# Packing every ninth sample with masked multiply-adds on VectorE, to the last channel, in a convolve-and-whiten kernel

## The chip, the cores and the metric

The kernel runs on one core of one Trainium2 chip. The metric is the device time of one execution in microseconds (us); less is better. The engines named below are PE (TensorE), DVE (VectorE), ACT (ScalarE), POOL (GpSimd) and SP (SyncE, which here only issues DMAs). SBUF is the memory on the chip, with 128 partitions; PSUM is the memory into which PE writes, in eight banks.

## What is computed

The input x is [4 images, 64 channels, 256, 256] in float32. Two layers follow each other.

```python
# layer 0: a long 2-D convolution for each channel, with a separable kernel
hx = implicit_filter(z, X weights)            # small sine network, 256 taps x 64 channels
hy = implicit_filter(z, Y weights)
k  = einsum('ijk,imk->ijmk', hx, hy)[0]       # one 256x256 kernel per channel, an outer product
y  = irfft2(rfft2(x, 512) * rfft2(k, 512) / 512)[..., :256, :256]
x  = y + x * bias[:, None, None]

# layer 1: whitening over channels
x1   = transpose(x, (1, 0, 2, 3)).reshape(64, -1)       # channels x (image, row, column)
x1_s = x1[:, ::9]                                       # every ninth sample
mean1 = mean(x1_s, axis=-1)
cov  = x1_s @ x1_s.T / n + 0.01 * eye(64)
out  = newton_schulz_inverse_sqrt(cov, 5) @ (x1 - mean1)
```

## The kernel before

An image of one channel is held as 128 partitions x 2 row blocks x 256 columns: row b*128 + p lies in partition p, block b. Eight channels of one image are one x tile; there are four such tiles. The list `steps` holds 32 steps of (group g of eight channels, image n). The first 24 go through groups 0 to 5, all images of each; the last eight go image by image through groups 6 and 7. Inside a step the loop takes two channels at a time (c = 0, 2, 4, 6).

The convolution is two products with Toeplitz matrices on PE, one along each axis. `group` (products at L220) does the second product of one pair of channels and the first product of a pair two items later, so that PE always has both. The first product is copied to SBUF by ACT (L409). The second is added to x * bias by DVE (L412), which writes the result over x in its tile. The very first and last pairs have no partner, and are done alone by `half_group` (PE at L252, DVE's addition at L289). `store` then sends the result to DRAM in two DMAs on SP (y_d, L425).

**Packing.** The whitening needs every ninth sample, for a sum of products over samples. The sample that an index belongs to depends on image, row and column, so that in each partition and row block one residue s of 0 to 8 is the right first column. The tile samp of an image is [128, 2 blocks, 29 samples, 65] and holds in its last column ones. For each s, DVE copies the columns s, s + 9, ... of x into it where an integer mask for (partition, image, block, s) is not zero (COPY_PREDICATED, L319, in `pack_ops`). One operation takes both row blocks and eight channels (four in groups 6 and 7): nine operations a tile, or nine for each half of a tile.

These operations are not emitted at once. `store` puts them on a list, todo, with a planned cost, and `pack(time)` adds time to a credit and emits from the list until the credit is used up. `group` calls pack(2.92) at its end; at the very end each of the last two pairs calls pack(1.0) between `half_group` and `store`, and a last pack() empties the list. The cost of an operation is `0.3 + 1.5e-3 * H2 * NJ * channels`, with H2 = 2 and NJ = 29.

The last four channels of the last step are packed otherwise: `pack_by_pe` multiplies the tile's columns on PE with nine selection matrices (pick, the identity scaled by the mask, made on ACT at L135 in the second step), two channels at a time, and ACT (and DVE for one copy) bring the sums from PSUM into samp (L309, L311).

**After the loop.** `covariance(n)` sums the products of samp of image n on PE (L333). Images 0 to 2 have theirs inside the last steps, image 3 behind the loop. Products named spin (L442) are dummy matmuls on PE, two instructions each. `whitening` is a chain of small products and DVE/ACT operations that ends in the matrix W and a shift. Then 32 pieces of the stored convolution (2 MB each) are read back (yi, L357), multiplied by W (L635), shifted by ACT and DVE (L639, L640), and written out (L645). The first 13 read-backs take the places of tiles that are done with: nine are issued in the last steps of the loop and four behind the covariance in program order, all on SP's queue, behind the stores.

The order on each engine is the order of the program; nothing is reordered by a scheduler.

Of the kernel before, what the change touches and what calls it, by code (L numbers as in the profile page):

```python
# [37 lines left out]

F32 = mybir.dt.float32
I32 = mybir.dt.int32  # L40
AF = mybir.ActivationFunctionType
ALU = mybir.AluOpType
AX = mybir.AxisListType
# [2 lines left out]
NB, C, L = 4, 64, 256  # L46
P, H2 = 128, 2
EMB, ORDER = 33, 64
PIX = L * L
CG = 8  # L50
HP = P // 2
STEP = 9
NJ = 29
NSAMP = (NB * PIX + STEP - 1) // STEP
EPS = 0.01
N_ITER = 5
GW = P + L
FP = 4096

TURN = 6.283185  # L60
# [4 lines left out]
def conv_whiten_kernel(ctx: ExitStack, tc: tile.TileContext, a: dict, out: bass.AP):  # L65
    nc = tc.nc
    x = a["x"]

    const = ctx.enter_context(tc.tile_pool(name="const", bufs=1))
# [6 lines left out]
    psA = ctx.enter_context(tc.tile_pool(name="psA", bufs=8, space=bass.MemoryType.PSUM))  # L76

    y_d = [dram.tile([H2 * C, PIX // H2], F32, tag=f"y{n}", name=f"y_d{n}") for n in range(NB)]
    g_d = dram.tile([P, GW], F32, tag="g", name="g_d")
    g0_d = dram.tile([2 * CG, GW], F32, tag="g0", name="g0_d")  # L80

# [12 lines left out]
    wbd = scratch[:, 0:2, :].rearrange("p a w -> p (a w)")[:, 0 : 3 * P]  # L94
    nc.sync.dma_start(out=wbd, in_=a["wbd"])
    decay = scratch[:, 15, :]
    mask = const.tile([P, NB, H2, STEP], I32, tag="mask", name="mask")
    bias = const.tile([P, C], F32, tag="bias", name="bias")

    def load_x(t, g, n, c):  # L100
# [6 lines left out]
    steps = [(g, n) for g in range(C // CG - 2) for n in range(NB)]  # L107
# [10 lines left out]
    ident = const.tile([P, P], F32, tag="ident", name="ident")  # L118
    make_identity(nc, ident)
    samp = []  # L120
    for n in range(NB):
        t = spool.tile([P, FP], F32, tag="samp", name=f"samp{n}")
        samp.append(
# [3 lines left out]
        nc.gpsimd.memset(samp[n][:, :, NJ - 1, 0:C], 0.0)  # L127


    rows = const.tile([P, STEP], F32, tag="rows", name="rows")  # L130
    pick = const.tile([P, STEP, P], F32, tag="pick", name="pick")

    def load_pick(lo, hi):
        for s in range(lo, hi):
            nc.scalar.activation(pick[:, s, :], ident, AF.Copy, scale=rows[:, s : s + 1])  # L135

    taps = scratch[:, 11:13, :].rearrange("p a w -> p (a w)")[:, 0:GW]
    nc.gpsimd.memset(taps[:, L:GW], 0.0)  # L140

# [35 lines left out]
    nc.sync.dma_start(out=g0_d[0:CG], in_=taps[0:CG])  # L177
    nc.scalar.dma_start(out=g0_d[CG:], in_=taps[ORDER : ORDER + CG])
    nc.gpsimd.dma_start(out=g_d, in_=taps)
    nc.gpsimd.tensor_copy(rows, mask[:, NB - 1, 0, :])  # L180
    busy(22)

    def new_toeplitz(g):
# [4 lines left out]
    def load_toeplitz(t, g, f, half, lo=0, hi=CG, issue=nc.sync):  # L188
# [7 lines left out]
                tensor=source.tensor,  # L196
                offset=source.offset + row * GW + skip,
                ap=[[1, HP], [GW, hi - lo], [1, L - skip]],
            ),
# [91 lines left out]
                        ALU.mult, ALU.add,  # L291
                    )

    def pack_by_pe(g, n, yt, cs):

        pk = psA.tile([P, H2, cs.stop - cs.start, NJ], F32, tag="psA", name=f"pk_{cs.start}")
        for s in range(STEP):
            for b in range(H2):
                nj = (L - s + STEP - 1) // STEP
                nc.tensor.matmul(  # L300
                    pk[:, b, :, 0:nj],
                    lhsT=pick[:, (s - b) % STEP, :],
                    rhs=yt[:, cs, b, s : s + STEP * (nj - 1) + 1 : STEP],
                    start=(s == 0 and b == 0),
                    stop=(s == STEP - 1 and b == H2 - 1),
                    skip_group_check=True,
                )
        dst = samp[n][:, :, :, g * CG + cs.start : g * CG + cs.stop]
        nc.scalar.copy(dst[:, 0], pk[:, 0].rearrange("p c j -> p j c"))  # L309
        copy = nc.vector.tensor_copy if cs.stop == CG else nc.scalar.copy  # L310
        copy(dst[:, 1], pk[:, 1].rearrange("p c j -> p j c"))  # L311

    def pack_ops(g, n, yt, cs):
        def op(s):
            nj = (L - s + STEP - 1) // STEP
            src = yt[:, cs, :, s : s + STEP * (nj - 1) + 1 : STEP].rearrange("p c b j -> p b j c")
            dst = samp[n][:, :, 0:nj, g * CG + cs.start : g * CG + cs.stop]
            m = mask[:, n, :, s : s + 1].unsqueeze(3).to_broadcast([P, H2, nj, cs.stop - cs.start])
            nc.vector.copy_predicated(dst, m, src)  # L319

        cost = 0.3 + 1.5e-3 * H2 * NJ * (cs.stop - cs.start)
        return [(cost, lambda s=s: op(s)) for s in range(STEP)]

    cov = const.tile([P, C + 1], F32, tag="cov", name="cov")
    nc.gpsimd.memset(cov, 0.0)
# [38 lines left out]
    todo = []  # L364
# [55 lines left out]
    def store(second):  # L420
        g, n, c, yt, _ = second
        halves = g >= C // CG - 2
        for b in range(H2):
            row = b * C + g * CG + c
            nc.sync.dma_start(  # L425
                out=y_d[n][row : row + 2, :].rearrange("c (p w) -> p c w", w=L),
                in_=yt[:, c : c + 2, b],
            )

        if c == CG - 2 and (g, n) != steps[-1]:  # L430
            todo.extend(pack_ops(g, n, yt, slice(CG // 2 if halves else 0, CG)))
        elif c == CG // 2 - 2 and halves:
            todo.extend(pack_ops(g, n, yt, slice(0, CG // 2)))
# [3 lines left out]
    def spin(times):  # L437

        p = psA.tile([P, P], F32, tag="psA", name=f"spin{len(spins)}")
        spins.append(p)  # L440
        for _ in range(times):
            nc.tensor.matmul(p, lhsT=ident, rhs=ident, start=True, stop=True)  # L442
# [114 lines left out]
    with tc.manual_schedule(  # L557
        engines={engines.PE, engines.SP, engines.DVE, engines.Activation, engines.Pool}
    ):
        toep = {0: new_toeplitz(0)}  # L560

        for f, lo, hi in ((0, 0, 2), (0, 2, 4), (0, 4, 6), (1, 0, 2), (0, 6, 8), (1, 2, 4), (1, 4, 8)):
            for half in range(2):
                load_toeplitz(toep[0], 0, f, half, lo, hi, nc.scalar if half else nc.sync)
        for c in range(0, CG, 2):
            load_x(x_tiles[1], *steps[1], c)
        for i, (g, n) in enumerate(steps):
            xt = x_tiles[i % 4]
            for c in range(0, CG, 2):
                item = (g, n, c, xt, [])  # L570
                if g == C // CG - 1 and n > 0 and c == 2:
                    covariance(n - 1)
                if len(pending) == 2:
                    group(item, pending.pop(0))
                else:
                    half_group(item, 0)
                pending.append(item)
                if i == 0 and c == 6:

                    fold = const.tile([P, C], F32, tag="fold", name="fold")  # L580
                    nc.vector.tensor_tensor(fold, ident[:, 0:C], ident[:, C:P], ALU.add)

                    nc.scalar.activation(bf[:, 0:1], samp[0][:, 0, 0, C : C + 1], AF.Sqrt)
                if i == 1 and c < CG - 2:
                    load_pick(c // 2 * 3, c // 2 * 3 + 3)

                if i + 2 < len(steps):
                    load_x(x_tiles[(i + 2) % 4], *steps[i + 2], c)
                if (i, c) in blocks:
                    tg, part = blocks[i, c]  # L590
                    if part == 0:
                        toep[tg] = new_toeplitz(tg)
                    lo = part % 2 * CG // 2
                    load_toeplitz(toep[tg], tg, part // 4, part // 2 % 2, lo, lo + CG // 2)
                for _ in range(early.get((i, c), 0)):
                    load_next()
        g, n, c, yt, _ = pending[0]
        for item in pending:
            half_group(item, 1)
            pack(1.0)  # L600
            store(item)

        pack()
        i15 = place(2 * C, rows=C).rearrange("p (u c) -> p u c", u=2)
        for u in range(2):
            nc.gpsimd.tensor_scalar(i15[:, u], ident[0:C, 0:C], 1.5, None, ALU.mult)  # L606
        ones = place(P, rows=C)
        nc.gpsimd.memset(ones, 1.0)
        for lo in range(CG // 2, CG, 2):
            pack_by_pe(g, n, yt, slice(lo, lo + 2))  # L610
        spin(4)
        covariance(NB - 1)
        while len(loaded) < len(homes):
            load_next()
        W, shift = whitening(i15, ones)
# [3 lines left out]
    for i, (n, q) in enumerate(pieces):  # L619
        yt = loaded.pop(i)  # L620
# [5 lines left out]
        for w in range(FP // 1024):  # L626
# [6 lines left out]
            for k in range(2):  # L633
                for u in range(2):
                    nc.tensor.matmul(  # L635
                        po[u][halves[k]], lhsT=W[halves[u]], rhs=v[halves[u], k, cols],
                        start=True, stop=True,
# [12 lines left out]
def _constants():  # L650


    import numpy as np

    t = np.linspace(0.0, 1.0, L).astype(np.float32)
    lo, hi = math.log(0.01) / 1.5, math.log(0.01) / 0.3
    deltas = np.linspace(lo, hi, C).astype(np.float32)
    d = np.exp(-(t[None, :] * np.abs(deltas)[:, None]).astype(np.float64))
    decay = np.concatenate([d / (2 * L), d])[:, ::-1].astype(np.float32)
    p, n, b, s = np.ogrid[0:P, 0:NB, 0:H2, 0:STEP]  # L660
    mask = ((n * PIX + (b * P + p) * L + s) % STEP == 0).astype(np.int32)
    return {"decay": decay, "mask": mask}


# [41 lines left out]
```

## Time and profile before

| | us |
|---|---|
| median of 3 runs | 903.47 |
| lowest and highest run | 902.69, 903.47 |
| span of the profiled execution, first to last instruction | 902.1 |
| PE busy | 781.2 |
| DVE busy | 581.5 |
| ACT busy | 395.5 |
| POOL busy | 14.5 |
| COPY_PREDICATED at L319, 351 instructions | 297.2 |
| selection products at L300, 72 instructions | 8.3 |

The profiled execution's own time is not listed apart; the runs lie 0.6 to 1.4 us above its span.

The page of the profile gives, for 40 equal slices of the span, each engine's busy share in tenths (9 is 90% or more), the clock granted to PE (PEclk) and the DMA engines' share. The chain that ended last is followed back from the last instruction, at each step to what released it; a line of it in order of time has the start, the length, what ran, and how many instructions. A line of the timeline has the start and length of a run of like instructions on one engine, with their count. A line of the windows has, for one stretch, its length, then the busy time and number of instructions of PE, PEld, DVE, ACT and POOL, then the granted clock, the DMA share and GB/s.

### The profile page before, as it was taken

How to read it: one execution, taken by the hardware profiler on the slowest of the kernel's cores; microseconds unless marked ns; L12 is line 12 of the kernel's file. 1: busy time of each engine (PE TensorE's matmuls, PEld its weight loads, DVE VectorE, ACT ScalarE, POOL GpSimd, SP SyncE). 2: the span in 40 equal slices, each digit the busy share in tenths (PEclk: the TensorE clock that was granted, in tenths of full speed). 3: DMA queues.
4: the chain of work that ended last, by engine and by line, in shares of the span. 5: the costliest groups of instructions: out<-in, count | busy, mean ns of one | idle time of the engine just before them, and what ended most of it. 6: DMA issues, size and time to landing. Idle time of an engine off the chain costs nothing.

```text
span 902.1 us, 28046 instructions
## 1 busy us (share of the span) xinstructions
PE 781.2 (87%) x11928; PEld 647.5 (72%) x11928; DVE 581.5 (64%) x801; ACT 395.5 (44%) x676; POOL 14.5 (2%) x40
## 2 busy tenths in 40 slices
PE   8999999999999999999999999999999565666200
PEld 7999999999999999999999999999533111212000
DVE  3487778877888778877888877877688332233200
ACT  2655554545455555545454444442487232233200
POOL 1000000000000000000000000000010000000000
PEclk9999999999999999999999999999999766866755
DMA  7988889798788888888997899979999999999998
GB/s 209 327 262 252 242 261 271 234 273 251 247 263 261 244 264 259 258 250 267 293 275 241 285 351 356 335 237 390 375 401 429 430 432 432 429 434 430 430 430 355
DMA packets 117912, 285.61 MB, mean 317 GB/s; under 512 B 8891, under 2 KB 91116, under 8 KB 110108
## 3 DMA queue, kind: packets, MB, share of 16 engines
q1 hardware_dynamic: 113436, 244.94, 79.0%
q0 software_dynamic: 3056, 37.95, 10.0%
q8 instruction: 95, 1.56, 0.7%
q10 hardware_dynamic: 1296, 0.93, 0.4%
q14 instruction: 29, 0.24, 0.1%
HBM read 149.35 MB, written 134.44 MB: 315 GB/s over the span
## 4 chain that ended last, share of the span: by engine, by line
PE 74%; DMA 11%; another core or an unknown queue 7%; DVE 0%; issue 0%; SPq 0%; ACT 0%; POOLq 0%; DVEq 0%
PE p L220 64%; DMA out_dram<-yi 5%; DMA yi<-y_d 5%; PE po L635 4%; PE pc L333 2%; PE ph L252 1%; PE pk L300 1%; PE spin L442 1%; DMA toep<-g_d 0%; PE busy L152 0%; PE pm L158 0%; SPq L357 0%; DMA scratch<-in_zw_dram 0%; DVE yi L640 0%
## 5 line engine op out<-in xcount | busy, mean ns | idle before, releaser
L220 PE MATMUL p<-toep,x 64*64 64x64 f32 (+3 forms) x5040 | 579.5, 284 | 0.8 <-issue 0.8
L220 PE MATMUL p<-toep,o 64*64 64x64 f32 (+3 forms) x5040 | 579.5, 284 | 0.0
L220 PEld LDWEIGHTS p<-toep,x 64*128 64x128 f32 (+1 forms) x5040 | 535.7, 166 | 24.4 <-issue 1.3
L220 PEld LDWEIGHTS p<-toep,o 64*128 64x128 f32 (+1 forms) x5040 | 536.7, 166 | 10.7 <-issue 0.2
L409 ACT COPY o<-p 64x512 f32<-64x512 f32 x504 | 292.8, 581 | 294.2 <-PE p L220 286.6
L319 DVE COPY_PREDICATED samp<-mask,x 128x464 f32<-128x464 int32 (+3 forms) x351 | 297.2, 847 | 9.8 <-DVE x L412 0.2
L412 DVE SCALAR_TENSOR_TENSOR x<-x,bias,p 128x512 f32<-128x512 f32 x252 | 179.8, 744 | 121.3 <-PE p L220 117.3
L635 PE MATMUL po<-yi,chain 64*64 64x512 f32 x1024 | 143.7, 720 | 60.4 <-DMA yi<-y_d 60.4
L640 DVE TENSOR_SCALAR yi<-po,shift 128x512 f32<-128x512 f32 x128 | 96.1, 751 | 109.0 <-PE po L635 100.7
L635 PEld LDWEIGHTS po<-yi,chain 64*64 64x64 f32 x1024 | 48.0, 162 | 155.2 <-issue 150.5
L639 ACT ACTIVATE yi<-po,shift 128x512 f32<-128x512 f32 x128 | 88.0, 687 | 116.7 <-PE po L635 116.0
L333 PE MATMUL pc<-samp 128*64 128x65 f32 x464 | 14.9, 223 | 0.0
L333 PEld LDWEIGHTS pc<-samp 128*64 128x64 f32 x464 | 14.3, 137 | 0.3
L645 POOL DMA_DIRECT2D out_dram<-yi x19 | 10.5, 554 | 130.5 <-DMA out_dram<-yi 55.1
L606 POOL TENSOR_SCALAR chain<-ident 64x64 f32<-64x64 f32 x2 | 1.0, 519 | 606.6 <-PE ph L252 606.6
L286 DVE COPY o<-ph 64x256 f32<-64x256 f32 x8 | 3.4, 422 | 9.7 <-PE ph L252 9.6
L152 PE MATMUL busy<-idle 128*128 128x128 f32 x64 | 9.4, 307 | 0.0
L152 PEld LDWEIGHTS busy<-idle 128*128 128x128 f32 x64 | 8.9, 222 | 0.2 <-issue 0.2
L300 PE MATMUL pk<-x,pick 128*128 128x56 f32 (+1 forms) x72 | 8.3, 292 | 0.0
L300 PEld LDWEIGHTS pk<-x,pick 128*128 128x128 f32 x72 | 8.1, 192 | 0.1
L442 PE MATMUL spin<-ident 128*128 128x128 f32 x50 | 7.9, 292 | 0.0
L286 ACT COPY o<-ph 64x256 f32<-64x256 f32 x8 | 2.9, 368 | 10.7 <-DMA toep<-g_d 9.2
(93 smaller groups left out, 77.4 us busy)
## 6 DMA issues: line engine op xcount, KB each, us to landing
x<-in_x_dram SPq DMA_DIRECT2D x128, 512.0 KB, 5.3
y_d<-x SPq DMA_DIRECT2D x256, 256.0 KB, 3.5
yi<-y_d SPq DMA_DIRECT2D x32, 2048.0 KB, 15.6
out_dram<-yi POOLq DMA_DIRECT2D x17, 2048.0 KB, 67.7
out_dram<-yi SPq DMA_DIRECT2D x11, 2048.0 KB, 32.9
toep<-g_d SPq DMA_DIRECT2D x28, 256.0 KB, 6.3
toep<-g_d SPq DMA_DIRECT2D x29, 192.0 KB, 5.7
out_dram<-yi SPq DMA_DIRECT2D x4, 1024.0 KB, 32.8
```

The lines of the kernel that those rows point to most:

```text
L152: nc.tensor.matmul(p, lhsT=idle[:, 0:P], rhs=idle[:, P : 2 * P], start=True, stop=True)
L220: mm = nc.tensor.matmul(ps[q : q + w, m, HP * k : L], lhsT=src[parts, k // 2, m * P + q : m * P + q + w], rhs=t[parts, : stop : -1] if k e ...
L300: nc.tensor.matmul(pk[:, b, :, 0:nj], lhsT=pick[:, (s - b) % STEP, :], rhs=yt[:, cs, b, s : s + STEP * (nj - 1) + 1 : STEP], start=(s == 0 ...
L319: nc.vector.copy_predicated(dst, m, src)
L333: nc.tensor.matmul(pc[half], lhsT=samp[n][:, b, j, 0:C], rhs=samp[n][:, b, j, :], start=(b == 0 and j < 2), stop=(b == H2 - 1 and j >= NJ ...
L409: nc.scalar.copy(o1[to], units[u][0][0][fr])
L412: nc.vector.scalar_tensor_tensor(x2[:, c2 + u], x2[:, c2 + u], bias[:, ch : ch + 1], units[u][1][0], ALU.mult, ALU.add,)
L442: nc.tensor.matmul(p, lhsT=ident, rhs=ident, start=True, stop=True)
L635: nc.tensor.matmul(po[u][halves[k]], lhsT=W[halves[u]], rhs=v[halves[u], k, cols], start=True, stop=True,)
L639: nc.scalar.activation(v[:, 0, cols], po[0], AF.Identity, bias=shift)
L640: nc.vector.tensor_scalar(v[:, 1, cols], po[1], shift, None, ALU.add)
L645: issue.dma_start(out=o[:, :, end - part : end], in_=v[:, :, end - part : end])
```

## The change

The mask becomes float32 (0.0 or 1.0). The packing of one residue s is split by row block, and is no longer a predicated copy: for s = 0 the columns times the mask are written into samp, and for each later s the columns times the mask are added to what is there. An operation has half the elements and there are 18 in the place of 9. The planned costs are new. The last four channels of the last step are packed in the same way, two channels at a time, when their store is emitted; the selection matrices and their products are gone. Behind the last pack() stand 16 spins in the place of the products and 4 spins.

```diff
+PACK_FIXED, PACK_EACH = 0.1, 1.05e-3
+SPINS = 16
...
-    mask = const.tile([P, NB, H2, STEP], I32, tag="mask", name="mask")
+    mask = const.tile([P, NB, H2, STEP], F32, tag="mask", name="mask")
...
-    rows = const.tile([P, STEP], F32, tag="rows", name="rows")
-    pick = const.tile([P, STEP, P], F32, tag="pick", name="pick")
-
-    def load_pick(lo, hi):
-        for s in range(lo, hi):
-            nc.scalar.activation(pick[:, s, :], ident, AF.Copy, scale=rows[:, s : s + 1])
...
-    nc.gpsimd.tensor_copy(rows, mask[:, NB - 1, 0, :])
...
-    def pack_by_pe(g, n, yt, cs):
...
     def pack_ops(g, n, yt, cs):
-        def op(s):
+        def op(s, b):
             nj = (L - s + STEP - 1) // STEP
-            src = yt[:, cs, :, s : s + STEP * (nj - 1) + 1 : STEP].rearrange("p c b j -> p b j c")
-            dst = samp[n][:, :, 0:nj, g * CG + cs.start : g * CG + cs.stop]
-            m = mask[:, n, :, s : s + 1].unsqueeze(3).to_broadcast([P, H2, nj, cs.stop - cs.start])
-            nc.vector.copy_predicated(dst, m, src)
-
-        cost = 0.3 + 1.5e-3 * H2 * NJ * (cs.stop - cs.start)
-        return [(cost, lambda s=s: op(s)) for s in range(STEP)]
+            src = yt[:, cs, b, s : s + STEP * (nj - 1) + 1 : STEP].rearrange("p c j -> p j c")
+            dst = samp[n][:, b, 0:nj, g * CG + cs.start : g * CG + cs.stop]
+            m = mask[:, n, b, s : s + 1]
+            if s == 0:
+                nc.vector.tensor_scalar(dst, src, m, None, ALU.mult)
+            else:
+                nc.vector.scalar_tensor_tensor(dst, src, m, dst, ALU.mult, ALU.add)
+
+        cost = PACK_FIXED + PACK_EACH * NJ * (cs.stop - cs.start)
+        return [(cost, lambda s=s, b=b: op(s, b)) for s in range(STEP) for b in range(H2)]
...
-        if c == CG - 2 and (g, n) != steps[-1]:
+        if (g, n) == steps[-1] and c >= CG // 2:
+            todo.extend(pack_ops(g, n, yt, slice(c, c + 2)))
+        elif c == CG - 2:
             todo.extend(pack_ops(g, n, yt, slice(CG // 2 if halves else 0, CG)))
...
-                if i == 1 and c < CG - 2:
-                    load_pick(c // 2 * 3, c // 2 * 3 + 3)
...
-        for lo in range(CG // 2, CG, 2):
-            pack_by_pe(g, n, yt, slice(lo, lo + 2))
-        spin(4)
+        spin(SPINS)
         covariance(NB - 1)
```

More of the change, by code (lines that the diff above doesn't have):

```diff
@@ L39 @@
 F32 = mybir.dt.float32
-I32 = mybir.dt.int32
 AF = mybir.ActivationFunctionType
@@ L292, in half_group @@
                     )
-    def pack_by_pe(g, n, yt, cs):
[L296 to L311, printed above, removed]
     def pack_ops(g, n, yt, cs):
-        def op(s):
+        def op(s, b):
             nj = (L - s + STEP - 1) // STEP
-            src = yt[:, cs, :, s : s + STEP * (nj - 1) + 1 : STEP].rearrange("p c b j -> p b j c")
-            dst = samp[n][:, :, 0:nj, g * CG + cs.start : g * CG + cs.stop]
-            m = mask[:, n, :, s : s + 1].unsqueeze(3).to_broadcast([P, H2, nj, cs.stop - cs.start])
-            nc.vector.copy_predicated(dst, m, src)
-        cost = 0.3 + 1.5e-3 * H2 * NJ * (cs.stop - cs.start)
-        return [(cost, lambda s=s: op(s)) for s in range(STEP)]
+            src = yt[:, cs, b, s : s + STEP * (nj - 1) + 1 : STEP].rearrange("p c j -> p j c")
[7 more added lines that the diff above has]
+        return [(cost, lambda s=s, b=b: op(s, b)) for s in range(STEP) for b in range(H2)]
     cov = const.tile([P, C + 1], F32, tag="cov", name="cov")
@@ L660, in _constants @@
     p, n, b, s = np.ogrid[0:P, 0:NB, 0:H2, 0:STEP]
-    mask = ((n * PIX + (b * P + p) * L + s) % STEP == 0).astype(np.int32)
+    mask = ((n * PIX + (b * P + p) * L + s) % STEP == 0).astype(np.float32)
     return {"decay": decay, "mask": mask}
```

## The prediction

> **What bounds the kernel now.** I read the page first (engines, slices), then the chain that ended last in order of time, then fine windows around its joints, then the timeline of VectorE there. Slices 2 to 27 show PE at 9; slices 29 to 39 show DMA at 9. So a PE stage is followed by a DMA stage, and the chain shows the joint:
>
> ```profile
> 599.72 13.88 PE p L220 x240
> 613.60 5.79 PE ph L252 x57
> 619.39 8.21 PE pk L300 x72
> 627.60 0.92 PE spin L442 x8
> 628.52 3.66 PE pc L333 x116
> ...
> 643.25 27.70 PE po L635 x256
> ```
>
> Seven pieces at L220 sum to 579.3 us for 126 groups, 4.60 us a group. The change touches nothing that PE does there. It replaces 619.39 to 628.52 (pk and 4 spins, 9.13 us).
>
> Whether that joint matters is asked of the windows (length, PE, PEld, DVE, ACT and POOL busy, PEclk, DMA share, GB/s):
>
> ```profile
> 632.18:643.25 11.07, 9.92 (x76) 8.10 (x78) 5.34 (x28) 2.08 (x11) 0.00 (x0) 1.00 1.00 425
> 643.25:644.00 0.75, 0.75 (x9) 0.29 (x12) 0.00 (x0) 0.00 (x0) 0.00 (x0) 1.00 1.07 459
> 644.00:646.00 2.00, 2.00 (x24) 0.77 (x20) 1.50 (x2) 1.38 (x2) 0.00 (x0) 1.00 0.49 201
> 646.00:648.00 2.00, 2.00 (x24) 0.65 (x20) 1.70 (x3) 1.62 (x3) 0.00 (x0) 1.00 0.60 222
> 648.00:650.00 2.00, 2.00 (x24) 0.72 (x20) 1.79 (x3) 1.66 (x3) 0.00 (x0) 1.00 1.02 382
> ```
>
> Through the whitening the DMA engines read back the convolution; they run dry near 644, and the first output goes out at 645.57. From 648 on they are full to the end. So a later W moves the end one for one, and an earlier W gains at most the hole: (1 - 0.49) x 2 + (1 - 0.60) x 2 = 1.8 us.
>
> **Part by part: the loop.** A full-width step had 9 COPY_PREDICATED of 448 or 464 elements (973, 1008 ns) and gets 18 multiply-adds of 224 or 232. No such row exists: two SBUF tensors, a scalar read per partition, strided. The rows nearest in kind are pointer-scalar multiply-adds. L412 (512 elements, 2 in 1.41 us, mean 744 ns) starts every 0.66 us, which is 512/0.96 ns + 0.13; L289 (256, 4 in 1.65 us, mean 473 ns) every 0.39, or + 0.125; L503 to L504 (64) 0.20, or + 0.135. (The pace is the length of the merged line less one mean, over one fewer than its count.)
>
> ```profile
> 635.99 0.28 DVE L503 SCALAR_TENSOR_TENSOR chain<-chain,chain 64x64 f32<-64x64 f32 x1
> 636.19 0.24 DVE L504 TENSOR_SCALAR chain<-chain 64x64 f32<-64x64 f32 x1
> ```
>
> I take 0.125 + N/960 us: 0.367 for 232, 0.246 for 116, 0.185 for 58. Below, L534 to L535 (64, no pointer) gives 0.14, so 0.135 for 58; above is COPY_PREDICATED itself, 627 ns for 232. With mine VectorE has 4 x 1.33 + 18 x 0.367 = 11.9 us in four groups (18.4 us), where it had 4 x 1.33 + 9 x 0.99 = 14.2. The planner now puts 9 operations behind one group: 9 x 0.367 + 1.33 = 4.6, one group's time. PSUM has eight banks and a group takes four, so L412 may be about 3.3 us late before PE feels it. Cost zero; the cover is those 3.3 us.
>
> Also at nothing: the nine pick scalings (3.0 us) leave ACT in the second step, where ACT waits on PE; the rows cast leaves POOL's queue; the mask has the same bytes. The x loads on SP wait for packing that ends no later than now.
>
> **The tail, which sets the end.** VectorE's order today:
>
> ```profile
> 613.28 1.40 DVE L412 SCALAR_TENSOR_TENSOR x<-x,bias,p 128x512 f32<-128x512 f32 x2
> 614.59 2.55 DVE L319 COPY_PREDICATED samp<-mask,x 128x224 f32<-128x224 int32 x4
> 617.02 1.65 DVE L289 SCALAR_TENSOR_TENSOR x<-x,bias,ph 128x256 f32<-128x256 f32 x4
> 618.59 1.30 DVE L319 COPY_PREDICATED samp<-mask,x 128x232 f32<-128x232 int32 x2
> 619.78 1.64 DVE L289 SCALAR_TENSOR_TENSOR x<-x,bias,ph 128x256 f32<-128x256 f32 x4
> 621.34 4.55 DVE L319 COPY_PREDICATED samp<-mask,x 128x232 f32<-128x232 int32 x7
> ```
>
> I ran the planner's credit by hand with the new costs (0.222 for four channels, 0.161 for two). Credit 2.92 releases 14 operations of 112 or 116 elements at 614.59, the first 1.0 releases the other 4, the second 1.0 releases 6 of the 18 for channels 4 and 5; the last pack() empties 12 and the 18 for channels 6 and 7. So 36 small operations stand behind the last L289. At my paces: 14 take 3.4 to 618.0; four L289 at 0.39 to 619.6; 4 take 1.0 to 620.6; four L289 to 622.2; 36 x 0.185 = 6.7 to 628.9; its result 0.1 later, 629.0. Today the covariance starts at 628.52: **+0.5**. At 0.135 it would start near 626.3 (-2.2).
>
> PE's cover is 16 spins, 32 instructions at 0.115 (8 in 0.92): 619.39 to 623.1. Then the covariance waits for VectorE's last operation instead of ACT's and VectorE's copies out of pk, with all of the whitening queued behind it, and PE idles 5.9 us (3.3 at the fast pace), which it nowhere does between the first steps and 702. What that does to the clock is shown later in the trace, in windows of 3.41 us:
>
> ```profile
> 701.62:705.03 3.41, 0.72 (x8) 0.00 (x0) 1.45 (x2) 1.27 (x2) 0.53 (x1) 1.00 1.05 452
> 705.03:708.44 3.41, 0.05 (x4) 0.08 (x5) 0.00 (x0) 0.00 (x0) 0.00 (x0) 0.50 0.99 423
> 708.44:711.86 3.42, 3.42 (x17) 1.11 (x21) 0.75 (x1) 0.69 (x1) 0.00 (x0) 0.50 1.00 426
> 711.86:715.27 3.41, 1.89 (x20) 0.46 (x12) 2.25 (x3) 2.06 (x3) 0.53 (x1) 1.00 1.04 447
> ```
>
> A window that is busy for less than about half (0.72 of 3.41) is followed by one at half clock; full clock returns after a nearly full window. A hole of 5.9 us leaves such a window wherever the boundaries fall, so the covariance starts at half clock and loses 1.35 us (a partial slow window) to 3.0 (nearly two); over all positions about 2.2. **+2.2.** Even the 3.3 us hole costs some 1.9.
>
> The Trainium skill, page "TensorE: Matmul & The Clock Gate", section "Part 1: The HAM clock gate", wants at least one idle window of about 3.4 us before the clock halves. By that stricter rule the 5.9 us hole holds one in some 73% of positions (an estimate), and the sum would be about +2.1 in place of +2.7; the 0.72 us row above halved without one, so the row decides.
>
> The page "VectorE: DVE Perf Modes", section "The TRN2 errata", prices an SBUF operation at 58 + N cycles and warns that many small tiles pay the fixed part each time. That would be 0.121 us for 58 elements, a covariance 2.7 us earlier, and about -1.2 with the clock; L503's 0.20 for 64 speaks for more, and decides.
>
> Behind the covariance nothing changes. On SP the last stores, and the read-backs queued behind them, wait for the last L289, some 0.9 us later; these reads were done 1.5 us before an output needed the engines, and W comes later by more. Sum: 0.5 + 2.2 = **+2.7 us**. The span is 902.1 and the runs 902.69 to 903.47, so 0.6 to 1.4 lies around the span; on the median, 906.2.
>
> **Rivals.**
> - The clock does not fall, or what is lost is made good by a pace nearer 0.16: the chain stays within 0.6 of today's, near 903.6. For it: the hole may be shorter. Against: the 705.03 row.
> - Faster: pace 0.135 and full clock. The chain is 2.2 shorter, capped by the 1.8 hole: 901.7. It decides only if the 36 end before about 626 and the hole stays under some 2 us. Against: every pointer-scalar row starts 0.125 or more above its elements.
> - Serial operations: each multiply-add waits for the one in front. L500 to L501, dependent, are 0.31 apart for 64 elements. The 36 then take 11.0 and end near 635.4, +6.9, with the clock +9.1: 912.6. Against: the two row blocks alternate, so only every second one depends, and 0.31/2 is under 0.185.
> - Strides make an operation as slow as COPY_PREDICATED (0.66 apart for 232): two bursts make L412 4.6 late against 3.3, 1.3 us for each of 24 steps, 935. Against: L311, 58 strided elements, takes 222 ns, like the 64 contiguous of L524 (218).
>
> **How the numbers follow.** A measurement here can tell about 0.2%, 1.8 us, from no change. Forecast case 0.62, range -0.3 (fast pace with clock loss) to +3.5, three quarters of it beyond 1.8: slower 0.46, same 0.16. Clock holds or pace pays 0.17, same. Faster 0.08. Serial 0.10, strides 0.03, both slower. Together faster 0.08, same 0.33, slower 0.59. The range takes the forecast and the even case, 902.3 to 908.0, its upper end one beyond the forecast's 907.0 towards the serial case.
>
> **What would show it.** COPY_PREDICATED gone; 738 packing operations, VectorE's busy time down from 581 to about 515; L220 still 579 us of chain. In the tail: packing on VectorE unbroken to about 629, PE idle 5 to 6 us behind the spins, PEclk 0.50 in the covariance, which takes 5 to 6.5 us where it took 3.66, and the first output matmul near 646. Wrong if PE waits inside L220, if the covariance runs at full clock, or if 58 elements cost under 0.14 or over 0.25 us.

## The result, and the profile after

The changed kernel takes 908.52 us (median of 4 runs, 908.29 to 909.61) against 903.08 for the kernel before in the same comparison (4 runs, 902.05 to 903.47). The ratio is 1.0065, with a 95% interval of 1.005 to 1.0079: slower by 5.4 us. The sign is the forecast's, the size is twice its 2.7, and the time lies outside its range.

The first view is the page of the changed kernel: busy time of the engines, and the costliest group of the packing (count, then busy us, mean ns of one, and the idle time ahead of them).

```profile
PE 780.0 (86%) x11880; PEld 642.9 (71%) x11880; DVE 608.8 (67%) x1187; ACT 391.7 (43%) x664; POOL 13.9 (2%) x39
...
L297 DVE SCALAR_TENSOR_TENSOR samp<-x,mask,samp 128x224 f32<-128x224 f32 (+5 forms) x656 | 301.4, 533 | 0.0
```

The packing has the 738 operations of the forecast (656 here and 82 at L295), but VectorE's busy time rose from 581.5 to 608.8 us, where a fall to about 515 was forecast. That is the first sign of where the sum was off. The big product of the loop is as it was: 63.8% of the changed chain stands at L214 (L220 before), 578.3 us against 579.3.

The second view is the chain that ended last, in order of time, from the last products of the loop to the first product of the output.

```profile
611.91 0.76 DVE x L390
...
617.29 1.56 DVE x L283 x4
...
620.17 1.56 DVE x L283 x4
621.74 0.36 DVE samp L295 x2
622.10 3.50 DVE samp L297 x16
625.60 0.35 DVE samp L295 x2
625.95 3.31 DVE samp L297 x15
629.26 0.14 issue
629.39 5.03 PE pc L311 x116
...
645.66 4.43 PE po L611 x37
```

The chain runs through VectorE from the end of the loop to the covariance: the two half-group additions (L283) with packing ahead of and between them, then 36 operations behind the last, as the forecast had put them. Those 36 take 7.5 us, not 6.7.

The third view is the windows around that joint (length; PE, PEld, DVE, ACT, POOL busy; granted clock, DMA share, GB/s).

```profile
622.05:625.46 3.41, 0.00 (x0) 0.00 (x0) 3.41 (x17) 0.00 (x0) 0.00 (x0) 1.00 0.98 309
625.46:628.87 3.41, 0.00 (x0) 0.00 (x0) 3.41 (x17) 0.00 (x0) 0.00 (x0) 0.50 0.97 415
628.87:632.29 3.42, 2.90 (x54) 2.93 (x56) 0.60 (x3) 0.00 (x0) 0.00 (x0) 0.50 1.02 436
644.00:646.00 2.00, 2.00 (x15) 1.48 (x18) 0.57 (x2) 0.47 (x2) 0.00 (x0) 1.00 0.13 49
646.00:648.00 2.00, 2.00 (x24) 0.77 (x20) 0.81 (x2) 1.10 (x2) 0.00 (x0) 1.00 0.01 4
648.00:650.00 2.00, 2.00 (x24) 0.68 (x20) 1.92 (x3) 1.65 (x3) 0.00 (x0) 1.00 0.36 131
```

PE is empty behind its 16 spins, the clock goes to 0.50, and the covariance begins in a slow window and takes 5.03 us for 3.66. From 644 to 650 the DMA engines, which were at 0.49, 0.60 and 1.02 before, stand at 0.13, 0.01 and 0.36: they wait for W.

The end of the loop differs from run to run, so the joints are compared from there. Both kernels were profiled a second time (r_before 902.39 us, r_after 908.74):

> The kernel before once more, for a second profile. If the first profile (span 902.1) was an early loop end with late gaps, its span comes nearer to 901, with W earlier than 643.25 by the same; if spans differ by the drain of the last writes (2.4 us from the last half MB to the last packet in the first profile), W stays and the drain changes.

> The changed kernel once more, for a second profile. The drain of the last writes took 4.05 us in the first against 2.42 in before. If the drain is chance: another value between 2.4 and 5.1 (e1 had 5.1, e3 2.7), with the span following it. If it belongs to the change: 4 again. The covariance again at half clock at its start, with a loss between 1.35 and 3.0.

| | loop ends | covariance starts, takes | first output product | span | from there to the end |
|---|---|---|---|---|---|
| before | 613.60 | 628.52, 3.66 | 643.25 | 902.1 | 258.9 |
| before, again | 611.83 | 626.75, 3.66 | 641.49 | 900.6 | 259.1 |
| after | 611.91 | 629.39, 5.03 | 645.66 | 906.5 | 260.8 |
| after, again | 612.05 | 629.55, 6.16 | 646.92 | 907.0 | 260.1 |

This is the chain of the kernel before, profiled again:

```profile
611.83 5.79 PE ph L252 x57
617.62 8.21 PE pk L300 x72
625.83 0.92 PE spin L442 x8
626.75 3.66 PE pc L333 x116
...
641.49 8.72 PE po L635 x77
```

The profile that the prediction was worked from had a loop that ended 1.8 us later than this one. Counted from the loop's end, the covariance starts at 14.9 before, in both profiles, and at 17.5 after, in both: **2.6 us later**. At half clock the covariance then loses **1.4 us in one profile and 2.5 in the other**. Together the first output product comes 4.1 and 5.2 us later (33.8 and 34.9 from the loop's end, against 29.7). The stretch behind it is longer too, by 1 to 2 us here. For the drain of the last writes the second profile lies between the two cases expected: over the last 12 us of the span the DMA engines are busy for a share of 0.59 and then 0.65 after, against 0.73 and 0.71 before, so the longer drain came again, but smaller. This part is taken up again below.

### The profile page after: what moved, and what is told of

Same layout as the page of the kernel before. It is cut to its first block, busy times and chain, and to the rows that moved or that the text cites. A ratio compares the mean times of both kernels' runs of the same rounds, so it can differ in the third digit from the quotient of the medians.

```text
span 906.5 us, 28318 instructions
## 1 busy us (share of the span) xinstructions
PE 780.0 (86%) x11880; PEld 642.9 (71%) x11880; DVE 608.8 (67%) x1187; ACT 391.7 (43%) x664; POOL 13.9 (2%) x39
## 4 chain that ended last, share of the span: by engine, by line
PE 72%; another core or an unknown queue 11%; DMA 8%; DVE 2%; SPq 0%; issue 0%; ACT 0%; DVEq 0%; POOLq 0%
PE p L214 64%; DMA out_dram<-yi 5%; PE po L611 4%; PE pc L311 2%; DMA yi<-y_d 2%; DVE samp L297 1%; PE ph L246 1%; PE spin L422 0%; SPq L335 0%; DMA toep<-g_d 0%; DVE x L283 0%; PE busy L147 0%; PE pm L153 0%; DMA scratch<-in_zw_dram 0%
## 5 line engine op out<-in xcount | busy, mean ns | idle before, releaser
L214 PE MATMUL p<-toep,x 64*64 64x64 f32 (+3 forms) x5040 | 578.5, 284 | 0.4 <-issue 0.4
L214 PE MATMUL p<-toep,o 64*64 64x64 f32 (+3 forms) x5040 | 578.6, 284 | 0.0
L214 PEld LDWEIGHTS p<-toep,x 64*128 64x128 f32 (+1 forms) x5040 | 535.3, 166 | 24.0 <-issue 0.7
L214 PEld LDWEIGHTS p<-toep,o 64*128 64x128 f32 (+1 forms) x5040 | 536.3, 166 | 10.6
L297 DVE SCALAR_TENSOR_TENSOR samp<-x,mask,samp 128x224 f32<-128x224 f32 (+5 forms) x656 | 301.4, 533 | 0.0
L611 PE MATMUL po<-yi,chain 64*64 64x512 f32 x1024 | 147.8, 738 | 58.9 <-DMA yi<-y_d 58.9
L295 DVE TENSOR_SCALAR samp<-x,mask 128x232 f32<-128x232 f32 (+2 forms) x82 | 28.6, 390 | 1.6
L422 PE MATMUL spin<-ident 128*128 128x128 f32 x74 | 10.6, 287 | 0.1
L422 PEld LDWEIGHTS spin<-ident 128*128 128x128 f32 x74 | 8.9, 191 | 0.8 <-DVE x L283 0.3
```

Of the source, the lines that this page charges most:

```text
L214: mm = nc.tensor.matmul(ps[q : q + w, m, HP * k : L], lhsT=src[parts, k // 2, m * P + q : m * P + q + w], rhs=t[parts, : stop : -1] if k e ...
L295: nc.vector.tensor_scalar(dst, src, m, None, ALU.mult)
L297: nc.vector.scalar_tensor_tensor(dst, src, m, dst, ALU.mult, ALU.add)
L611: nc.tensor.matmul(po[u][halves[k]], lhsT=W[halves[u]], rhs=v[halves[u], k, cols], start=True, stop=True,)
```

## The experiments

The theory (T) going in: the end of the packing is late because the small strided operations cost more than was taken, PE idles, the clock falls, and all of it goes through to the end; the loop costs nothing. The rival (R): the loop's own packing delays something, in the loop or through the order on VectorE.

**The loop's packing alone (e1_loop_only).** The changed kernel with the old end: selection products for the last four channels and 4 spins. Against the changed kernel the main lines are these; the selection matrices and `pack_by_pe` are back as they were before, and not shown.

```diff
-        if (g, n) == steps[-1] and c >= CG // 2:
-            todo.extend(pack_ops(g, n, yt, slice(c, c + 2)))
-        elif c == CG - 2:
+        if c == CG - 2 and (g, n) != steps[-1]:
...
-        spin(SPINS)
+        for lo in range(CG // 2, CG, 2):
+            pack_by_pe(g, n, yt, slice(lo, lo + 2))
+        spin(4)
```

> The changed packing in the loop, with the end of before: selection products on PE for channels 4 to 7 of the last step, then 4 spins. Theory T (the whole loss lies behind the loop: VectorE's small operations there are dearer than I took them, and the clock falls): the end is PE's again, so 901.5 to 904.5, against before's 903.1; VectorE still busier than before in the loop, and L214-like product time in the chain still 578 to 580. Rival R (VectorE's longer packing in the loop, 2 ns an element, is what costs): the loss stays, 906 or more.

Measured: 912.13 us, ratio 1.0105 (1.0091 to 1.0119), slower than the whole change. That is far outside what the theory gave, and on the rival's side (906 or more). The loop was not slowed (PE's product takes 578.7 us there). What happened is in the chain, and in the windows, of this kernel:

```profile
619.07 13.75 PE pk L304 x72
...
634.65 3.91 PE pc L340 x116
```

```profile
618.08:621.49 3.41, 2.56 (x22) 2.33 (x21) 3.41 (x11) 0.00 (x0) 0.69 (x3) 1.00 0.98 396
621.49:624.90 3.41, 3.41 (x18) 3.41 (x18) 0.79 (x3) 0.00 (x0) 0.00 (x0) 0.50 1.07 351
624.90:628.32 3.42, 3.42 (x18) 3.42 (x18) 0.00 (x0) 0.34 (x2) 0.00 (x0) 0.50 1.00 390
```

The dearer packing holds up the half-group addition, which the selection products wait for; PE idles 0.85 us in a window that is still busy for 2.56 of 3.41. The clock halves all the same, and four windows full of thin products (58 wide, from 621.49 to 635.07) do not bring it back: the selection products take 13.75 us instead of 8.21. So this run is no clean measure of the loop's cost; it shows that a short hole ahead of thin products is dear.

The Trainium skill, page "TensorE: Matmul & The Clock Gate", section "Part 1: The HAM clock gate", has the clock fall after at least one idle window of about 3.4 us; the changed kernel has one (622.05 above), but here no window was idle, and the measurement decides.

**Cover for the hole (e2_spins48).** In the changed kernel:

```diff
-SPINS = 16
+SPINS = 48
```

> The changed kernel with 48 spins for 16: 96 instructions at 0.115, 11.0 us, which cover PE's hole to about the start of the covariance. T: the clock stays at 1.00, the covariance takes 3.66 in the place of 5.03, W is 1.4 earlier, and so is the end: 906.8 to 907.4. If the lost clock doesn't reach the end: 908.5 as the changed kernel. If the spins run past VectorE's last operation, the gain is less by as much.

Measured: 906.56 us, ratio 1.0049 (1.0036 to 1.0061). That is 2.0 less than the change's 908.52. Each against the kernel before in its own comparison, it is 4.0 against 5.4, so 1.5 less; the two intervals overlap, and the size is better read from the trace. The windows that were empty, and the covariance in the chain:

```profile
622.05:625.46 3.41, 3.41 (x33) 3.41 (x32) 3.41 (x17) 0.00 (x0) 0.00 (x0) 1.00 1.14 380
625.46:628.87 3.41, 3.26 (x30) 3.06 (x28) 3.41 (x17) 0.00 (x0) 0.00 (x0) 1.00 0.96 403
```

```profile
629.49 3.70 PE pc L311 x116
```

VectorE ends at the same time, the clock stays at 1.00, and the covariance has its 3.7 us back, where it took 5.03 and 6.16. The clock term is shown: in the trace it is worth 1.3 and 2.5 us on the covariance.

**The order within an operation (e3_order).** Source and destination are walked with the samples innermost in place of the channels.

```diff
-            src = yt[:, cs, b, s : s + STEP * (nj - 1) + 1 : STEP].rearrange("p c j -> p j c")
-            dst = samp[n][:, b, 0:nj, g * CG + cs.start : g * CG + cs.stop]
+            src = yt[:, cs, b, s : s + STEP * (nj - 1) + 1 : STEP]
+            dst = samp[n][:, b, 0:nj, g * CG + cs.start : g * CG + cs.stop].rearrange("p j c -> p c j")
```

> The changed kernel, but each packing operation runs through its elements samples first (36 bytes apart in x, 260 in samp), channels outside, where the change runs channels first (2 KB apart in x, 4 bytes in samp). Same elements, same count of operations. If the 2 ns an element come from the steps of the addresses in that order: 58 elements fall from 0.22 to about 0.16 to 0.19 and 232 from 0.57 to about 0.37, VectorE's busy time falls by some 80 to 100 us, the covariance starts some 2 us earlier and the end is 905.5 to 907. If they come from reading two SBUF tensors in a multiply-add whatever the order: the same paces, 908 to 909.

Measured: 909.03 us, ratio 1.0072 (1.0058 to 1.0086); an operation of 58 elements starts every 0.23 us, no less than the change's 0.22, and one of 232 takes 658 ns where the change has 637. Which of the strides runs innermost is not the cause.

**Contiguous on one side, on both (e5_near_src, e6_near_dst, e7_near_both).** The same operations, sizes and counts as the change, at other addresses, so that the packed samples are the wrong ones or lie in the wrong places. Of the three edits, this is that of e7_near_both. e5_near_src changes the addresses of the source alone (29 neighbouring columns of each channel, walked samples first as in e3_order), e6_near_dst those of the destination alone.

```diff
-            src = yt[:, cs, b, s : s + STEP * (nj - 1) + 1 : STEP].rearrange("p c j -> p j c")
-            dst = samp[n][:, b, 0:nj, g * CG + cs.start : g * CG + cs.stop]
+            w = cs.stop - cs.start
+            src = yt[:, cs.start, b, 0 : nj * w].rearrange("p (j c) -> p j c", c=w)
+            flat = samp[n][:, b].rearrange("p j c -> p (j c)")
+            at = (g * CG + cs.start) * NJ
+            dst = flat[:, at : at + nj * w].rearrange("p (j c) -> p j c", c=w)
```

> The changed kernel, where a packing operation reads neighbouring samples of x (4 bytes apart, so the wrong samples) in the order channels, samples; writes and counts as in the change. If the step of the reads of x makes the 2 ns an element: 58 elements fall from 0.22 to 0.17 to 0.19, 232 from 0.57 to about 0.37. If not: 0.22 and 0.57.

> The changed kernel, where a packing operation reads x as the change does, and reads and writes one contiguous piece of samp (the wrong places). If the step of samp makes the 2 ns: 0.17 to 0.19 for 58, 0.37 for 232. If not: 0.22 and 0.57.

> The changed kernel with x and samp both read and written contiguously (the wrong samples, in the wrong places). If any step makes the 2 ns: 0.37 for 232. If a multiply-add on two SBUF tensors with a scalar per partition takes 2 ns an element as such: 0.57 still.

Measured, one run each: 907.5, 906.84 and 902.93 us, beside 902.60 for the kernel before. The groups of 232 elements, by form, in the changed kernel and then in these three:

```profile
L297 DVE SCALAR_TENSOR_TENSOR samp<-x,mask,samp 128x232 f32<-128x232 f32 x144 | 80.6, 637 | 0.0
```

```profile
L297 DVE SCALAR_TENSOR_TENSOR samp<-x,mask,samp 128x232 f32<-128x232 f32 x144 | 81.4, 644 | 0.0
```

```profile
L300 DVE SCALAR_TENSOR_TENSOR samp<-x,mask,samp 128x232 f32<-128x232 f32 x144 | 80.2, 631 | 0.0
```

```profile
L300 DVE SCALAR_TENSOR_TENSOR samp<-x,mask,samp 128x232 f32<-128x232 f32 x144 | 55.5, 455 | 0.0
```

One strided side is as dear as two; only with both contiguous does the price fall. The paces are read from VectorE's timeline, where like operations in a row are one line; two such lines of the changed kernel, then two of e7_near_both:

```profile
317.07 3.89 DVE L297 SCALAR_TENSOR_TENSOR samp<-x,mask,samp 128x232 f32<-128x232 f32 x7
622.01 3.59 DVE L297 SCALAR_TENSOR_TENSOR samp<-x,mask,samp 128x58 f32<-128x58 f32 x16
```

```profile
317.32 2.67 DVE L300 SCALAR_TENSOR_TENSOR samp<-x,mask,samp 128x232 f32<-128x232 f32 x7
620.41 3.11 DVE L300 SCALAR_TENSOR_TENSOR samp<-x,mask,samp 128x58 f32<-128x58 f32 x16
```

The pace is the length of such a line less one mean, over one fewer than its count. The mean of 232 elements stands above; that of 58 is 301 and 284 ns.

| elements | forecast | change | both contiguous |
|---|---|---|---|
| 232 | 0.367 | 0.54 | 0.369 |
| 58 | 0.185 | 0.22 | 0.188 |

With contiguous operands the forecast's formula holds within 0.004 us, and VectorE is busy for 517.6 us (515 forecast). Each further element costs (0.54 - 0.22)/174 = 1.8 ns strided, and (0.369 - 0.188)/174 = 1.04 ns contiguous. The prediction's serial rival is out too: in e7_near_both each operation still adds to what an earlier one wrote, as in the change, and the pace is the formula's. The times of these three kernels are no clean comparison: in e6_near_dst and e7_near_both the covariance reads other places, so it starts before the packing ends.

The Trainium skill, page "VectorE: DVE Perf Modes", section "The TRN2 errata", lists 58 + N cycles, an estimate of 0.121 us for 58 elements, and says itself that this row comes out too low for single operations. The runs show 0.188 contiguous and 0.22 strided, and decide.

**A later W and nothing else (e4_late_w).** In the kernel before:

```diff
-        spin(4)
+        spin(14)
```

> Before, with 14 spins for 4 in front of the last covariance: 20 more instructions on PE, 2.3 us at full clock, nothing else. T (DMA engines have run dry by then, so a later W moves the end one for one): 905.2 to 905.6 against 903.1. If the outputs catch up: 903 to 904. If a later W costs more than its delay, through the writes that drain last: over 906.

Measured: 906.37 us, ratio 1.004 (1.0027 to 1.0053), so 2.4 to 4.8 us more. From the loop's end W comes 2.2 us later (31.9 against 29.7), with PE at full clock. The median lies in the third of the cases expected (over 906), but the interval begins at 2.4, only 0.2 above those 2.2 us. From the first output product to the end it takes 259.5 us, where the kernel before took 258.9 and 259.1. So a later W is paid at least in full; how much more it costs than itself is not settled.

**Four channels at once by PE, with either loop (h2_four_before, h3_four_after).** Both kernels pack the last four channels with 36 selection products, 112 or 116 wide, in one set, and fill PE with spins ahead of it so that the clock stays up. h2 has the old loop:

```diff
-        for lo in range(CG // 2, CG, 2):
-            pack_by_pe(g, n, yt, slice(lo, lo + 2))
-        spin(4)
+        spin(9)
+        pack_by_pe(g, n, yt, slice(CG // 2, CG))
+        spin(3)
```

h3 has the changed loop, the same end, and 17 spins in the place of 9.

> Before, but the selection products take the last four channels in one set (36 instructions in the place of 72, twice as wide), behind 9 spins that wait out VectorE's last addition, then 3 spins. Products 621.4 to about 625.6, copies behind VectorE's last predicated copy at 626.0, covariance at 626.3 to 626.6 against 628.52: W 2 us earlier. T (one for one, no more than the 1.8 us hole): 900.6 to 901.6 against about 902.7. If the wider products cost twice as much each: no gain, 902 to 904.

> The same end (one set of selection products for four channels) behind the changed packing of the loop, with 17 spins in front, so that PE never idles. Only the loop's packing tells it from the kernel with four channels and predicated copies. T (the loop's packing costs nothing): within 1.5 us of that kernel, 900.5 to 903. Rival R (the loop's packing costs, through VectorE's or the DMA engines' time): 904 or more.

Measured: 904.41 us, ratio 1.0015 (1.0006 to 1.0024), and 907.16 us, ratio 1.0041 (1.0029 to 1.0054). h2 was meant as an improvement and is none: 36 wide products take 7.4 us, 0.205 apart, where 72 thin ones take 8.2, 0.114 apart, and the set starts only when all four channels are there. The pair gives the price of the loop's packing with the clock at 1.00: 907.16 - 904.41 = 2.75 us, so here the rival holds and not the theory. It isn't paid inside the loop. Most of it is in the timelines of VectorE of h2 and then of h3, the second half-group addition:

```profile
618.89 1.65 DVE L289 SCALAR_TENSOR_TENSOR x<-x,bias,ph 128x256 f32<-128x256 f32 x4
```

```profile
620.77 1.69 DVE L293 SCALAR_TENSOR_TENSOR x<-x,bias,ph 128x256 f32<-128x256 f32 x4
```

Both loops end at about the same time (612.7 and 612.6), but the addition is 1.9 us later in h3. The planned cost of a 112 or 116 wide operation is 0.222, its pace is 0.33; a credit of 2.92 therefore lets 14 of them, 4.7 us, in front of the additions. Another 0.7 lies between the first output product and the end (259.2 in h2, 259.9 in h3).

**More instructions on VectorE (e8_dots).** The 0.8 us could come from the number of instructions that VectorE runs. In the kernel before, a one-element write stands behind each predicated copy but the last step's, 342 more instructions:

```diff
+    dot = const.tile([P, 1], F32, tag="dot", name="dot")
...
             nc.vector.copy_predicated(dst, m, src)
+            if (g, n) != steps[-1]:
+                nc.vector.memset(dot, 0.0)
```

> Before, with one more tiny VectorE instruction (a memset of one element per partition) behind each predicated copy but those of the last step: 342 more, near the 386 that the change adds, VectorE some 25 us busier, nothing else. From the first output product to the end, kernels with the old packing took 259.0 to 259.6 us and those with the new one 259.7 to 260.9. If the count of VectorE instructions makes that 0.8: 260 here, and the end 903.3 to 903.8 against about 902.7. If not: 259.0 to 259.6, and no change, within 0.8 of before.

Measured: 902.56 us, ratio 1.0001 (0.9992 to 1.001), and 259.1 us behind the first output product. The count is not the cause.

**What stays open.** Over the nine profiles with the new packing in the loop, the stretch from the first output product to the end (span less its start) takes 259.6 to 260.8 us, mean 260.0; over the five with the old, 258.9 to 259.5, mean 259.1. The runs speak against three causes: the count of instructions (e8_dots, 259.1), a late W (e4_late_w, 259.5; e7_near_both has an early W, 641.25, and still 260.0), and the memory freed by the selection matrices (e1_loop_only and h3_four_after keep them, 259.8 and 259.9). The windows over the last 12 us of the span, here of before and then of after, show where most of it lies:

```profile
890.10:902.10 12.00, 0.00 (x0) 0.00 (x0) 0.00 (x0) 0.00 (x0) 0.00 (x0) 0.50 0.73 299
```

```profile
894.50:906.50 12.00, 0.00 (x0) 0.00 (x0) 0.00 (x0) 0.00 (x0) 0.00 (x0) 0.50 0.59 242
```

Over the nine profiles the DMA engines are busy there for a share of 0.59 to 0.71, mean 0.65, and over the five for 0.70 to 0.73, mean 0.71. That is about 0.7 us more of idle time while the last writes drain. What makes the drain longer was not found.

## Why the prediction was right in its direction and wrong in its size

*Removed and added work.* Right: 738 packing operations, the loop's product unchanged on PE (578.3 against 579.3). The cover held more narrowly than was thought: at 0.54 for 232 elements, nine operations and a group's additions take 9 x 0.54 + 1.33 = 6.2 us against a group's 4.6, which by this sum (it was not read from the trace) puts L412 some 3.2 us late after two bursts, against the 3.3 allowed. The rival in which strides make an operation as slow as COPY_PREDICATED had the right mechanism at 0.54 in place of 0.66, and no price in the loop. Its own sum was off: the 4.6 us late go by 0.62 an operation, and by the 0.66 that it states they would be 5.3.

*The order at the end.* Right: 14 operations, four additions, 4 operations, four additions, then 36, as worked out from the credit.

***The pace: the step that failed.*** "I take 0.125 + N/960 us: 0.367 for 232, 0.246 for 116, 0.185 for 58." Measured: 0.54, 0.33 and 0.22. From the loop's end the last half-group addition was to end 8.6 us later (622.2 - 613.60) and did so 9.8 later (621.74 - 611.91); the 36 were to take 6.7 and took 7.5 (629.26 - 621.74). That is 1.2 + 0.8 = 2.0 us, and with the rounding turns the term of +0.5 into the +2.6 measured. The formula itself was right, as e7_near_both shows; it was read from rows with contiguous operands. The argument that set the strides aside compared the duration of one operation with 58 strided elements with that of one with 64 contiguous ones. At 58 elements the slope is worth only 0.03 us of 0.22; on 232 it is 0.17. The only wide strided rows of the trace were COPY_PREDICATED's. With 232 elements it starts every 0.66 us, twice the 0.33 of the 116 here, and it was kept as an outer bound instead of being read as the nearest row.

*The stated limit did not catch it.* The prediction called itself wrong if 58 elements cost under 0.14 or over 0.25 us. They cost 0.22; the miss came as much from the 18 four-channel operations, for which no limit was given.

*The clock.* Right. PE idled from the end of its spins to the covariance, the covariance ran at 0.50 and lost 1.4 and 2.5 us, inside the 1.35 to 3.0 and around the 2.2 taken; e2_spins48 gave 1.5 to 2.0 back. The hole was 7.8 us (621.57 to 629.39), not 5 to 6, for the reason above. The rule that a window must be under half busy to be followed by half clock is too mild: in e1_loop_only a window busy for 2.56 of 3.41 was followed by one. That full clock returns after a nearly full window did not hold there either: four full windows of thin products passed at 0.50.

*One for one to the end.* Right within what these runs tell, with 0.8 us on top that the prediction did not have, most of it in the drain of the last writes and without a known cause. The sum as it should have stood is 2.6 + 1.4 to 2.5 + 0.8 = 4.8 to 5.9, and the medians differ by 5.4.

*The range* reached 908.0, one beyond the forecast's own upper end. COPY_PREDICATED's 0.66 for 232, with the same 0.125 ahead, is 2.3 ns an element: 0.39 for 116 and 0.26 for 58, which puts some 5.3 us more behind the loop. An estimate with half of that would have been 906.2 + 2.6 = 908.8; the bound was used for the loop and not for the end.

## What to carry to other kernels

Price an operation by a row with its access pattern and its width: fixed part and slope are separate, and a short row tells nothing of the slope. When work moves from an engine that was kept busy to another, put the waiting engine's clock into the sum, and keep it covered up to the moment the work arrives (here 48 spins in place of 16 were worth 1.5 to 2.0 us). Costs given to a planner by hand decide what stands in front of the critical operation; one that is a third too low let 1.9 us more of filler go first in h3_four_after.

## What was not expected of the hardware

- On VectorE a float32 multiply-add with a strided operand in SBUF, source or destination, costs about 1.8 ns an element (232: 0.54 us), with both contiguous about 1.04 (0.369). Replacing one predicated copy of both row blocks, 0.66 for 232 elements, by two multiply-adds of 116 at 0.33 saves VectorE nothing.
- On PE a selection product with a strided moving operand takes 0.114 us at 58 columns and 0.205 at 112 to 116, where a spin with 128 contiguous columns takes 0.115. Each of them loads its own 128 columns of weights, so what the 0.114 is due to is not shown; the 0.205 is dearer than the wider spin.
- A hole of 0.85 us on PE, followed by thin products that keep it busy, left the clock at 0.50 for four windows, 13.6 us.
